# One tile for each score, more idle transposes at the start, and a written order for the end of an attention and expert layer

## The chip, the cores and the metric

The kernel runs on one core of one Trainium2 chip. A core has five engines that run at the same time and wait for one another through semaphores: TensorE (PE in the profile, with PEld for its weight loads), VectorE (DVE), ScalarE (ACT), GpSimd (POOL) and SyncE (SP), which here only issues transfers. The metric is device microseconds of one execution. Before the change the median of three runs is 1106.41 us (1105.07 to 1107.13).

## The reference

One sequence of S = 1024 rows of H = 512 numbers, all in 32-bit floats, goes through an attention layer and a feed-forward layer, each between two layer norms:

```
x = x + norm(attention(norm(x)))
x = x + norm(ffn(norm(x)))

attention: 32 query heads, 8 key/value heads of 128 numbers, causal;
           scores = q k^T / sqrt(128); softmax over the keys; times v; times w_o
ffn:       base = x base_W^T + base_b
           p    = softmax(x router_W^T + router_b)      (15 routes, the best 8 kept)
           w[e] = sum of the kept p whose route maps to expert e
           out  = base + 2 * sum over e of ((x A_e^T) * w[e]) B_e
```

A norm takes the mean and the variance of a row of 512 numbers.

## The kernel before, in words

The rows are cut into 8 row tiles t of 128, and the heads into 8 groups g (one key/value head and its four query heads). A block is one (g, t). There are 64 blocks: groups 0 to 5 one after the other, and then groups 6 and 7 in turn, with the row tiles in the order 0 1, 6 7, 4 5, 2 3. The main loop (lines 798 to 829) goes over the blocks. In block i it makes the four scores tiles (i, j), j = 0 to 3; each holds 32 query rows of all four heads (128 partitions) against the n = 128 t + 32 (j + 1) keys that causality leaves. Between the four, PE is given a quarter each of other work: projections for later blocks, the weighted values of block i - 2, the output projection of earlier ones, and pieces of the feed-forward layer of row tiles that are complete.

One score goes like this (scores, line 404). PE multiplies into a PSUM tile s. DVE adds the causal mask to the last 32 columns (L426) and takes the maximum (L428), ACT takes the exponential with its sum (L433). When the next score has been multiplied, DVE takes the reciprocal of the sum (L439), ACT scales (L440), and DVE transposes blocks of 32 x 32 (L446) into a tile T. After the fourth score, 16 transfers bring T into the key-major tile K (L106, to_keys), and two blocks later PE multiplies K with the values (po).

[...] The pool ps_s has two tiles s of 1024 columns, two banks each; ps_m has three banks under the tag pm, for every product and transpose but po, which has one bank of its own. A row tile with t below 4 needs at most 512 columns. There the kernel puts two scores into one tile:

```
if t < TPB and j % 2:
    s = score_tile.pop(0)[:, QB:]
else:
    s = ps_s.tile([P, S], F32, tag="s", name=f"s_{name}")
    score_tile[0] = s
```

The order on an engine is either written or planned. PE's instructions, the loads and those of DVE and ACT in the score chain are pinned to program order (keep). The other instructions are placed by the framework's planner. Function order (line 95) pins an instruction as long as the main loop runs (score_tile is then not empty) and leaves it to the planner afterwards. The vector work of a row tile (norms, routing) is cut into steps; in the main loop they are put into a list (defer) and worked off one or more per score (work_off). After the main loop defer carries each step out at once, so that its instructions follow directly in the program, and the planner orders them.

What is left behind the last scores (lines 832 to 848) is: the weighted values and output projections of the last two blocks, and the feed-forward layer of the row tiles c = 4, d = 5, e = 2 and f = 3. For each row tile it runs project_o (sum pO onto acc, L489), ffn_norms (statistics, norm, add of x, statistics, norm to h), ffn_router (transpose of h to hT, product pl with router and A, softmax over 15 routes, and the step route, which picks the best 8 and scales, L614 to L631), ffn_out (four products of hT with base_W into pf, transpose of the scaled hw, product with B, the sum y with the bias, L659, its norm, and the add to acc, L665), and the store. The reciprocal root of every norm is a power on POOL (L228) between two steps of DVE. In this part pl, and pf of e and f, lie in halves of the tiles s (bank_ffn); the other products take pm banks.

At the start x is loaded, normed row tile by row tile on DVE, transposed by PE (input_turn) and copied to xnT by ACT (L264); 20 transposes of the identity matrix (idle, line 771), whose result nobody reads, run on PE before x is there.

Of the kernel before, what the change touches and what calls it, by code (L numbers as in the profile page):

```python
# [22 lines left out]
def kernel(  # L23
# [68 lines left out]
    def keep(ins):  # L92
        return tc.keep_in_program_order(ins)

    def order(ins):

        return keep(ins) if score_tile else ins

    def matmul(*args, **kw):
        keep(nc.tensor.matmul(*args, **kw))  # L100
# [115 lines left out]
    def layernorm(dst, src, name, by=nc.vector):  # L216

        got = []

        def statistics():  # L220
            stats = small.tile([P, 6], F32, tag="stats", name=f"stats_{name}")
            order(nc.vector.bn_stats(stats, src))
            mv = small.tile([P, 2], F32, tag="mv", name=f"mv_{name}")
            order(nc.vector.bn_aggr(mv, stats))
            ve = small.tile([P, 1], F32, tag="ve", name=f"ve_{name}")
            order(nc.vector.tensor_scalar(ve, mv[:, 1:2], EPS, None, ALU.add))
            rstd = small.tile([P, 1], F32, tag="rstd", name=f"rstd_{name}")
            order(nc.gpsimd.tensor_tensor(rstd, ve, neg_half, ALU.pow))  # L228
            got.extend((mv, rstd))

        def norm():
            mv, rstd = got
            if by is nc.vector:
                order(by.tensor_scalar(dst, src, mv[:, 0:1], rstd, ALU.subtract, ALU.mult))
                return
            shift = small.tile([P, 1], F32, tag="shift", name=f"shift_{name}")
            order(nc.vector.tensor_scalar(shift, mv[:, 0:1], rstd, -1.0, ALU.mult, ALU.mult))
            nc.scalar.activation(dst, src, AF.Identity, bias=shift, scale=rstd)

        return statistics, norm  # L240

    def bank(name):
        return ps_m.tile([P, 512], F32, tag="pm", name=name)

    spare = []

    def bank_ffn(name):

        if not score_tile:
            if not spare:  # L250
                both = ps_s.tile([P, S], F32, tag="s", name=f"s_{name}")
                spare.extend((both[:, :512], both[:, 512:]))
            return spare.pop(0)
        return bank(name)

    def bank_pv(name):
        return ps_m.tile([P, 512], F32, tag="po", name=name, bufs=1)
# [1 line left out]
    def transposed(dst, src, name):  # L259

        pt = bank(f"ptx_{name}")
        for c in range(KC):
            transpose(pt[:, ts(c, P)], src[:, ts(c, P)], ident)
        nc.scalar.copy(dst, pt.rearrange("p (c q) -> p c q", q=P))  # L264

    def input_norms(rows):

# [110 lines left out]
    score_tile = {}  # L378
    deferred = []

    def defer(*steps, first=False):

        if score_tile:
            deferred[:0] = steps if first else ()
            deferred.extend(() if first else steps)
        else:
            for step in steps:
                step()

    def work_off(most=1):  # L390
        for _ in range(min(most, len(deferred))):
# [12 lines left out]
    def scores(g, t, j):  # L404

        n = t * P + (j + 1) * SQ
        full = (t + 1) * P
        name = f"{g}_{t}_{j}"

        if t < TPB and j % 2:  # L410
            s = score_tile.pop(0)[:, QB:]
        else:
            s = ps_s.tile([P, S], F32, tag="s", name=f"s_{name}")
            score_tile[0] = s
        for c0 in range(0, n, QB):
            w = min(QB, n - c0)
            matmul(
                s[:, c0 : c0 + w],
                qTs[g, t // 2][:, (t % 2) * NSUB + j, :, :].rearrange("p h q -> p (h q)"),
                kTs[g, c0 // QB][:, :w],  # L420
                start=True,
                stop=True,
            )
        pin = keep if blocks.index((g, t)) >= N2 + 2 else lambda ins: ins
        rescale_scores()
        keep(nc.vector.tensor_tensor(s[:, n - SQ : n], s[:, n - SQ : n], smask, ALU.add))  # L426
        nmax = small.tile([P, 1], F32, tag="nmax", name=f"nmax_{name}")
        keep(nc.vector.tensor_reduce(nmax, s[:, :n], AX.X, ALU.max, negate=True))  # L428
        p = act.tile([P, S], F32, tag="p", name=f"p_{name}", bufs=3)
        if n < full:  # L430
            nc.gpsimd.memset(p[:, n:full], 0.0)  # L431
        total = small.tile([P, 1], F32, tag="total", name=f"total_{name}")
        keep(nc.scalar.activation(p[:, :n], s[:, :n], AF.Exp, bias=nmax, accum_out=total))  # L433
        finish_scores()
        work_off(1 + len(deferred) // 5)

        def rescale():
            rec = small.tile([P, 1], F32, tag="rec", name=f"rec_{name}")
            keep(nc.vector.reciprocal(rec, total))  # L439
            keep(nc.scalar.mul(p[:, :n], p[:, :n], rec))  # L440

        def finish():
            if j == 0:
                turned[g, t] = turn_view(turn_tile("T", g, t), t)
            pin(
                nc.vector.transpose(  # L446
                    turned[g, t][:, :, j, :, :].rearrange("p b k q -> p k b q"),
                    p[:, :full].rearrange("p (k b q) -> p k b q", b=R, q=SQ),
                )
            )  # L450
# [17 lines left out]
    def weighted_values(g, t):  # L468


        def finish(po):
            o = act.tile([P, R * P], F32, tag="attnT", name=f"attnT_{g}_{t}", bufs=3)
            attnT[g, t] = o
            nc.scalar.copy(o, po)  # L474
            keyed.pop((g, t))

        def term(k):
            p = keyed[g, t][:, :, :, k, :].rearrange("p h s q -> p (h s) q")
            return vs[g // GV, k][:, ts(g % GV, D)], p

        return chained(
            lambda: bank_pv(f"po_{g}_{t}"), [lambda k=k: term(k) for k in range(t + 1)], finish
        )
# [88 lines left out]

    def ffn_norms(t):

        by = nc.gpsimd if score_tile else nc.vector
        statistics, norm = layernorm(acc[t], acc[t], f"a{t}")

        def add_x():
# [7 lines left out]
            norm_h()  # L586
            state["h", t] = h

        defer(statistics, add_x, statistics_h, last)

    def ffn_router(t):

# [4 lines left out]

        def products():
            hT = state["hT", t]
            pl = bank_ffn(f"pl_{t}")[:, : NR + ER]  # L600
            for c in range(KC):
                matmul(pl, hT[:, c, :], ra_sb[:, c, :], start=(c == 0), stop=(c == KC - 1))
            lg = small.tile([P, NR], F32, tag="lg", name=f"lg_{t}")
# [2 lines left out]
            order(nc.vector.tensor_reduce(nmax, lg, AX.X, ALU.max, negate=True))  # L606
            ex = small.tile([P, NR], F32, tag="ex", name=f"ex_{t}")
            total = small.tile([P, 1], F32, tag="total", name=f"totalr_{t}")
            nc.scalar.activation(ex, lg, AF.Exp, bias=nmax, accum_out=total)
            defer(lambda: route(pl, ex, total), first=True)  # L610

        def route(pl, ex, total):
            rec = small.tile([P, 1], F32, tag="rec", name=f"recr_{t}")
# [27 lines left out]
    def ffn_out(t):  # L641
# [2 lines left out]

        def base(c):
            if c == 0:
                pf.append(bank_ffn(f"pf_{t}") if t in (e, f) else bank(f"pf_{t}"))
            matmul(pf[0], state["hT", t][:, c, :], weights["base", c], start=(c == 0), stop=False)

        def turn_hw():  # L650
            pt = bank(f"ptw_{t}")
            transpose(pt[:, :ER], state.pop(("hw", t)).rearrange("p e r -> p (e r)"), ident)
            hwT = state["hwT", t] = ffn.tile([ER, P], F32, tag="hwT", name=f"hwT_{t}")
            nc.scalar.copy(hwT, pt[:, :P])

        def finish():
            matmul(pf[0], state.pop(("hwT", t)), bt_sb, start=False, stop=True)
            y = ffn.tile([P, H], F32, tag="hy", name=f"y_{t}", bufs=3)
            order(nc.vector.tensor_tensor(y, pf[0], bias_bc, ALU.add))  # L659
            by = nc.vector if t in (e, f) else nc.gpsimd  # L660
            statistics, norm = layernorm(y, y, f"y{t}", nc.vector if t in (e, f) else nc.scalar)

            def add_y():
                norm()
                order(by.tensor_tensor(acc[t], y, acc[t], ALU.add))  # L665
                state["done", t] = True

            defer(statistics, add_y)

        w = [(512, lambda c=c: base(c)) for c in range(KC)]  # L670
        return w[:2], [(P, turn_hw)], w[2:], [(512, finish)]
# [68 lines left out]
    def run(pieces):  # L740
        for _, f in pieces:
            f()
# [25 lines left out]
    input_norms(range(TPB, NT))  # L768

    idle = bank("idle")  # L770
    for n in range(20):
        transpose(idle[:, ts(n % KC, P)], ident, ident)
    input_turn(0)
    run(project_v(0, 0))
    for t in range(1, 3):
        input_turn(t)
# [54 lines left out]

    rescale_scores()
    finish_scores()
    score_tile.clear()
    work_off(len(deferred))
    for t in (e, f):
        reload_x(t)
    (turn_d, products_d), (turn_e, products_e), (turn_f, products_f) = map(ffn_router, (d, e, f))
    out_c, out_d, out_e, out_f = map(ffn_out, (c, d, e, f))
    o_pair = project_o_pair(*pairs[N // 2 - 2])  # L840
    run([turn_d] + weave(o_pair[:8], attend(N - 2)) + [products_d] + o_pair[8:])
    run(out_c[0] + out_c[1] + out_c[2] + attend(N - 1))
    run(project_o(*blocks[N - 2]) + out_c[3] + project_o(*blocks[N - 1]))
    run(out_d[0] + out_d[1] + out_d[2] + [turn_e] + out_d[3] + [products_e])
    run(out_e[0] + out_e[2][:1] + [turn_f] + out_e[2][1:] + [products_f])
    run(out_f[0] + out_e[1] + out_f[2][:1] + out_e[3] + out_f[2][1:] + out_f[1] + out_f[3])
    for t in (*ready, c, d, e, f):
        ffn_store(t)


# [39 lines left out]
```

## Time and profile before

| What | Before |
|---|---|
| median of three runs | 1106.41 us |
| profiled execution, its own time | 1105.28 us |
| span of the profile, first to last instruction | 1103.5 us |
| mean granted clock of TensorE | 0.994 |
| PE busy | 1074.5 us, 97% |
| DVE busy | 654.0 us, 59% |
| ACT busy | 491.2 us, 45% |
| POOL busy | 113.8 us, 10% |
| last DVE instruction ends | 1100.31 us |
| moved by DMA | 111.82 MB |

A row of a group or of the order in time names the source line, the engine, the operation and its tiles (written <- read), with the shape; [x <- y] says how long the engine stood idle before it and what ended that. Matmuls overlap, so their rows last longer than the distance from one start to the next, which is what counts for throughput: one 128x512 matmul row lasts 592 ns, and the next starts 429 ns after it. Each product of 32-bit numbers is two such rows. Helpers record under their own line: every product of PE is L100, every transpose L103, every transfer L106, so work is told apart by tile names.

### The profile page before, as it was taken

To read this page: it belongs to the slowest core of one execution; us is meant where nothing else is said; L and a number is where in the kernel's file an instruction comes from. 1 tells how busy PE (TensorE), PEld (TensorE's weight loads), DVE (VectorE), ACT (ScalarE), POOL (GpSimd) and SP (SyncE) were. 2 spreads that over 40 slices of the span, in tenths; PEclk is the share of its full clock that TensorE was granted. 3 is DMA by queue.
4 is the path that set the end of the run, shared out by engine and by line. 5 is a ranking of instruction groups with operands and counts; after the bars stand their busy time and mean duration, and the time that the engine had idled before them with its cause. 6 is when DMAs were issued, how large, how long until landed. Compare 5 with 4: busy or idle time off the path is not lost.

```text
span 1103.5 us, 12827 instructions
## 1 busy us (share of the span) xinstructions
PE 1074.5 (97%) x3836; PEld 704.5 (64%) x3836; DVE 654.0 (59%) x1529; ACT 491.2 (45%) x991; POOL 113.8 (10%) x299
## 2 busy tenths in 40 slices
PE   8899999999999999999999999999999999999895
PEld 6676666666776666656676666666777556466452
DVE  4466555765465545766456654765446766566746
ACT  2554534554354434554354443555335554453501
POOL 2400012000020002000020000100020110111212
PEclk9999999999999999999999999999999999999998
DMA  5145342455125431454224441365333655444221
GB/s 181 40 107 141 67 115 58 125 144 115 24 68 155 107 82 45 113 144 105 52 60 125 121 104 37 93 176 123 86 102 100 166 144 116 127 107 104 68 67 38
DMA packets 79061, 111.82 MB, mean 101 GB/s; under 512 B 18176, under 2 KB 50560, under 8 KB 78992
## 3 DMA queue, kind: packets, MB, share of 16 engines
q1 hardware_dynamic: 52976, 82.08, 31.5%
q10 hardware_dynamic: 25040, 27.27, 7.9%
q0 software_dynamic: 976, 1.65, 0.6%
q8 instruction: 31, 0.51, 0.2%
q14 instruction: 38, 0.31, 0.1%
HBM read 33.34 MB, written 2.10 MB: 32 GB/s over the span
## 4 chain that ended last, share of the span: by engine, by line
PE 82%; DVE 7%; ACT 5%; DMA 2%; issue 1%; SPq 1%; POOL 1%; ACTq 0%; POOLq 0%; DVEq 0%
PE po L100 20%; PE s L100 18%; PE pq L100 16%; PE pk L100 4%; PE pv L100 4%; PE pe L100 4%; PE pa L100 3%; ACT p L433 2%; PE pO L100 2%; PE pc L100 2%; PE pb L100 2%; PE pd L100 2%; DVE T L446 2%; PE pf L100 2%; DVE nmax L428 2%; ACT p L440 2%
## 5 line engine op out<-in xcount | busy, mean ns | idle before, releaser
L100 PE MATMUL s<-kT,qT 128*128 128x512 f32 (+15 forms) x768 | 273.8, 465 | 8.7 <-ACT p L433 8.6
L100 PE MATMUL po<-K,v 128*128 128x512 f32 x576 | 277.3, 596 | 4.3 <-DMA K<-T 2.6
L433 ACT ACTIVATE p<-s,nmax 128x32 f32<-128x32 f32 (+31 forms) x256 | 179.2, 700 | 203.1 <-DVE nmax L428 197.9
L440 ACT ACTIVATE p<-p,rec 128x32 f32<-128x32 f32 (+31 forms) x256 | 187.9, 734 | 179.3 <-DVE rec L439 121.0
L446 DVE STREAM_TRANSPOSE T<-p 128x128 f32<-128x128 f32 (+7 forms) x256 | 198.2, 775 | 100.4 <-ACT p L440 89.4
L100 PE MATMUL pq<-xnT,wq 128*128 128x256 f32 x1024 | 235.7, 379 | 0.0
L100 PEld LDWEIGHTS s<-kT,qT 128*128 128x128 f32 x768 | 144.0, 190 | 137.4 <-issue 105.5
L100 PEld LDWEIGHTS pq<-xnT,wq 128*128 128x128 f32 x1024 | 192.8, 190 | 38.5 <-issue 16.5
L428 DVE TENSOR_REDUCE nmax<-s 128x1 f32<-128x32 f32 (+31 forms) x256 | 180.6, 705 | 8.2
L100 PEld LDWEIGHTS po<-K,v 128*128 128x128 f32 x576 | 107.8, 191 | 78.0 <-issue 63.3
L426 DVE TENSOR_TENSOR s<-s,smask 128x32 f32<-128x32 f32 x256 | 47.8, 187 | 132.2 <-PE s L100 131.5
L431 POOL MEMSET p<- 128x96 f32 (+2 forms) x192 | 29.7, 155 | 848.4 <-DVE T L446 782.9
L439 DVE RECIPROCAL rec<-total 128x1 f32<-128x1 f32 x256 | 39.8, 155 | 55.1 <-ACT p L433 53.2
L100 PE MATMUL pv<-wv,xnT 128*128 128x256 f32 x256 | 69.1, 388 | 0.9 <-ACT xnT L264 0.9
L350 ACT ACTIVATE qT<-pq 128x512 f32<-128x512 f32 x64 | 38.1, 595 | 71.1 <-PE pq L100 71.1
L474 ACT COPY attnT<-po 128x512 f32<-128x512 f32 x64 | 37.4, 584 | 63.2 <-PE po L100 63.0
L100 PE MATMUL pk<-xnT,wk 128*128 128x512 f32 x128 | 64.5, 593 | 0.0
L100 PE MATMUL pa<-wo,attnT 128*128 128x256 f32 x224 | 62.7, 390 | 0.0
L100 PEld LDWEIGHTS pv<-wv,xnT 128*128 128x128 f32 x256 | 49.1, 194 | 11.0 <-issue 2.7
L100 PEld LDWEIGHTS pa<-wo,attnT 128*128 128x128 f32 x224 | 41.6, 192 | 19.4 <-issue 14.5
L433 ACT ACTIVATION_READ_ACCUMULATOR p<-s,nmax 128x1 f32 x256 | 49.5, 193 | 0.0
L523 DVE TENSOR_TENSOR sums<-attnT 128x256 f32<-128x256 f32 x28 | 11.9, 425 | 56.8 <-ACT attnT L474 56.7
(120 smaller groups left out, 776.6 us busy)
## 6 DMA issues: line engine op xcount, KB each, us to landing
K<-T SPq DMA_DIRECT2D x128, 128.0 KB, 2.4
K<-T SPq DMA_DIRECT2D x128, 112.0 KB, 2.2
wq<-in_w_q_dram ACTq DMA_DIRECT2D x27, 512.0 KB, 4.8
K<-T SPq DMA_DIRECT2D x128, 96.0 KB, 2.2
K<-T SPq DMA_DIRECT2D x128, 80.0 KB, 2.1
K<-T SPq DMA_DIRECT2D x123, 64.0 KB, 2.0
wo<-in_w_o_dram ACTq DMA_DIRECT2D x28, 256.0 KB, 3.8
K<-T SPq DMA_DIRECT2D x123, 48.0 KB, 1.9
```

The source lines that it names most:

```text
L100: keep(nc.tensor.matmul(*args, **kw))
L350: nc.scalar.mul(qTs[g, u][:, :, j - 1 : j + 1, :].rearrange("p s h q -> p h s q"), pm[0].rearrange("p (h s q) -> p h s q", h=2, q=SQ), scale,)
L426: keep(nc.vector.tensor_tensor(s[:, n - SQ : n], s[:, n - SQ : n], smask, ALU.add))
L428: keep(nc.vector.tensor_reduce(nmax, s[:, :n], AX.X, ALU.max, negate=True))
L431: nc.gpsimd.memset(p[:, n:full], 0.0)
L433: keep(nc.scalar.activation(p[:, :n], s[:, :n], AF.Exp, bias=nmax, accum_out=total))
L439: keep(nc.vector.reciprocal(rec, total))
L440: keep(nc.scalar.mul(p[:, :n], p[:, :n], rec))
L446: nc.vector.transpose(turned[g, t][:, :, j, :, :].rearrange("p b k q -> p k b q"), p[:, :full].rearrange("p (k b q) -> p k b q", b=R, q=SQ),)
L474: nc.scalar.copy(o, po)
L523: nc.vector.tensor_tensor(s1, a21, a22, ALU.add)
```

## The change

Three things change. First, every score has a tile s of its own, in all row tiles; the two-in-one branch goes, and with it the spare halves (bank_ffn): pl is now always a pm bank, and pf of e and f takes a whole tile s each. Second, there are 26 idle transposes before the first input_turn in place of 20, and 4 more right behind it, ahead of the first value projection. Third, the part behind the last scores gets a written order: order and several ACT instructions are now pinned there, steps are put into one list per row tile (held), and calls go(...) place each step at a chosen point between PE's pieces. With that, the norm of y for row tile e goes from DVE to ACT, and its add from DVE to POOL. The stores of the row tiles that are ready are issued ahead of this part, and not after it.

```diff
     def order(ins):
-        return keep(ins) if score_tile else ins
+        return keep(ins)
...
-            nc.scalar.activation(dst, src, AF.Identity, bias=shift, scale=rstd)
+            act_norm = nc.scalar.activation(dst, src, AF.Identity, bias=shift, scale=rstd)
+            if held:
+                keep(act_norm)
...
-    def bank_ffn(name):
-        if not score_tile:
-            if not spare:
-                both = ps_s.tile([P, S], F32, tag="s", name=f"s_{name}")
-                spare.extend((both[:, :512], both[:, 512:]))
-            return spare.pop(0)
-        return bank(name)
...
+    held = {}
+
+    def defer(t, *steps, first=False):
+
+        if held:
+            held[t].extend(steps)
+            return
+        deferred[:0] = steps if first else ()
+        deferred.extend(() if first else steps)
+
+    def go(*rows):
+
+        for t in rows:
+            held[t].pop(0)()
...
-        if t < TPB and j % 2:
-            s = score_tile.pop(0)[:, QB:]
-        else:
-            s = ps_s.tile([P, S], F32, tag="s", name=f"s_{name}")
-            score_tile[0] = s
+        s = ps_s.tile([P, S], F32, tag="s", name=f"s_{name}")
...
-        by = nc.gpsimd if score_tile else nc.vector
+        by = nc.vector if held else nc.gpsimd
...
-            pl = bank_ffn(f"pl_{t}")[:, : NR + ER]
+            pl = bank(f"pl_{t}")[:, : NR + ER]
...
-                pf.append(bank_ffn(f"pf_{t}") if t in (e, f) else bank(f"pf_{t}"))
+                if t in (e, f):
+                    pf.append(ps_s.tile([P, S], F32, tag="s", name=f"pf_{t}")[:, :512])
+                else:
+                    pf.append(bank(f"pf_{t}"))
...
-            by = nc.vector if t in (e, f) else nc.gpsimd
-            statistics, norm = layernorm(y, y, f"y{t}", nc.vector if t in (e, f) else nc.scalar)
+            by = nc.vector if t == f else nc.gpsimd
+            statistics, norm = layernorm(y, y, f"y{t}", nc.vector if t == f else nc.scalar)
...
-    for n in range(20):
+    for n in range(26):
         transpose(idle[:, ts(n % KC, P)], ident, ident)
     input_turn(0)
+    for n in range(4):
+        transpose(idle[:, ts(n, P)], ident, ident)
     run(project_v(0, 0))
...
-    score_tile.clear()
     work_off(len(deferred))
+    held.update({t: [] for t in (c, d, e, f)})
     for t in (e, f):
         reload_x(t)
+    for t in ready:
+        ffn_store(t)
...
     run([turn_d] + weave(o_pair[:8], attend(N - 2)) + [products_d] + o_pair[8:])
+    go(d)
     run(out_c[0] + out_c[1] + out_c[2] + attend(N - 1))
-    run(project_o(*blocks[N - 2]) + out_c[3] + project_o(*blocks[N - 1]))
-    run(out_d[0] + out_d[1] + out_d[2] + [turn_e] + out_d[3] + [products_e])
+    run(project_o(*blocks[N - 2]))
+    go(e)
+    run(out_c[3])
+    go(e, e)
+    run(project_o(*blocks[N - 1]))
+    go(e, f, c, f, f)
+    run(out_d[0] + out_d[1] + out_d[2] + [turn_e] + out_d[3])
+    go(f, c)
+    run([products_e])
+    go(d, e)
     run(out_e[0] + out_e[2][:1] + [turn_f] + out_e[2][1:] + [products_f])
-    run(out_f[0] + out_e[1] + out_f[2][:1] + out_e[3] + out_f[2][1:] + out_f[1] + out_f[3])
-    for t in (*ready, c, d, e, f):
+    go(d, f)
+    run(out_f[0] + out_e[1] + out_f[2][:1] + out_e[3])
+    go(e)
+    run(out_f[2][1:] + out_f[1])
+    go(e)
+    run(out_f[3])
+    go(f, f)
+    for t in (c, d, e, f):
         ffn_store(t)
```

The four remaining ACT copies of this part (hT, attnT, hwT and the exponential of the router) are pinned in the same way as act_norm.

More of the change, by code (lines that the diff above doesn't have):

```diff
@@ L243, in bank @@
         return ps_m.tile([P, 512], F32, tag="pm", name=name)
-    spare = []
-    def bank_ffn(name):
-        if not score_tile:
-            if not spare:
-                both = ps_s.tile([P, S], F32, tag="s", name=f"s_{name}")
-                spare.extend((both[:, :512], both[:, 512:]))
-            return spare.pop(0)
-        return bank(name)
     def bank_pv(name):
@@ L263, in transposed @@
             transpose(pt[:, ts(c, P)], src[:, ts(c, P)], ident)
-        nc.scalar.copy(dst, pt.rearrange("p (c q) -> p c q", q=P))
+        copy = nc.scalar.copy(dst, pt.rearrange("p (c q) -> p c q", q=P))
+        if held:
+            keep(copy)
     def input_norms(rows):
@@ L379 @@
     deferred = []
[L381 to L385, printed above, removed]
-        else:
-            for step in steps:
-                step()
+    held = {}
+    def defer(t, *steps, first=False):
+        if held:
+            held[t].extend(steps)
[5 more added lines that the diff above has]
+            held[t].pop(0)()
     def work_off(most=1):
@@ L408, in scores @@
         name = f"{g}_{t}_{j}"
-        if t < TPB and j % 2:
-            s = score_tile.pop(0)[:, QB:]
-        else:
-            s = ps_s.tile([P, S], F32, tag="s", name=f"s_{name}")
-            score_tile[0] = s
+        s = ps_s.tile([P, S], F32, tag="s", name=f"s_{name}")
         for c0 in range(0, n, QB):
@@ L473, in finish @@
             attnT[g, t] = o
-            nc.scalar.copy(o, po)
+            copy = nc.scalar.copy(o, po)
+            if held:
+                keep(copy)
             keyed.pop((g, t))
@@ L587, in last @@
             state["h", t] = h
-        defer(statistics, add_x, statistics_h, last)
+        defer(t, statistics, add_x, statistics_h, last)
     def ffn_router(t):
@@ L608, in products @@
             total = small.tile([P, 1], F32, tag="total", name=f"totalr_{t}")
-            nc.scalar.activation(ex, lg, AF.Exp, bias=nmax, accum_out=total)
-            defer(lambda: route(pl, ex, total), first=True)
+            act_exp = nc.scalar.activation(ex, lg, AF.Exp, bias=nmax, accum_out=total)
+            if held:
+                keep(act_exp)
+            defer(t, lambda: route(pl, ex, total), first=True)
         def route(pl, ex, total):
@@ L653, in turn_hw @@
             hwT = state["hwT", t] = ffn.tile([ER, P], F32, tag="hwT", name=f"hwT_{t}")
-            nc.scalar.copy(hwT, pt[:, :P])
+            copy = nc.scalar.copy(hwT, pt[:, :P])
+            if held:
+                keep(copy)
         def finish():
@@ L666, in add_y @@
                 state["done", t] = True
-            defer(statistics, add_y)
+            defer(t, statistics, add_y)
         w = [(512, lambda c=c: base(c)) for c in range(KC)]
```

## The prediction

> **What bounds the kernel now.** I read the page first. TensorE (PE) is busy 97% of the span, so the time is PE's work plus PE's idle moments, and a change that removes no PE work can only win idle moments.
>
> ```profile
> PE 1074.5 (97%) x3836; PEld 704.5 (64%) x3836; DVE 654.0 (59%) x1529; ACT 491.2 (45%) x991; POOL 113.8 (10%) x299
> PEclk9999999999999999999999999999999999999998
> ```
>
> Next the list of who waited for whom, for PE alone (total us, times, longest):
>
> ```profile
> PE s L100 <- ACT p L433: 8.6, 17, 1.2
> PE po L100 <- DMA K<-T: 2.6, 1, 2.6
> PE s_pf L100 <- ACT hT L264: 1.5, 1, 1.5
> PE ptx_x L103 <- DVE K_x L282: 1.3, 1, 1.3
> PE s_pl L100 <- ACT hT L264: 1.0, 1, 1.0
> PE ptw L103 <- DVE y L659: 0.9, 1, 0.9
> ```
>
> The largest is a score matmul waiting for an exponential. Asked by window, the same row says 3.2 us in 4 waits between 26 and 62 us (group 0), 4.7 in 12 from 62 to 1035, 0.7 in one after 1035. Which exponential? One wait in order of time (start, us):
>
> ```profile
> 153.29 1.03 PE L100 MATMUL pq<-xnT,wq 128*128 128x256 f32 x4
> 154.49 0.39 ACT L433 ACTIVATE p<-s,nmax 128x160 f32<-128x160 f32 x1
> 154.78 0.19 ACT L433 ACTIVATION_READ_ACCUMULATOR p<-s,nmax 128x1 f32 x1
> 155.03 0.59 PE L100 MATMUL s<-kT,qT 128*128 128x192 f32 x2 [0.71 <-ACT p L433]
> ```
>
> The score of 192 columns (t=1, j=1) starts 0.06 us after the exponential of 160 columns (t=1, j=0): the score just before it, which sits in the other bank of the same tile. I matched all 17 waits to their scores: every one is an odd j with t below 4, no other kind of score waits. So half a tile is given only when the other half's reader has ended.
>
> Then the start, by windows (us; stretch, PE busy with its count, PEld, DVE, ACT, POOL, granted clock, DMA share, GB/s):
>
> ```profile
> 5.40:6.70 1.30, 0.01 (x1) 0.00 (x0) 1.23 (x5) 0.57 (x1) 0.92 (x2) 1.00 1.03 363
> 6.70:8.00 1.30, 0.66 (x4) 0.42 (x4) 1.23 (x4) 1.29 (x2) 0.99 (x5) 1.00 1.08 316
> 8.70:11.30 2.60, 2.60 (x8) 2.06 (x7) 2.04 (x9) 0.00 (x0) 0.79 (x1) 0.50 1.08 369
> ```
>
> PE sits still for most of 5.4 to 8.06 and the clock then goes to 0.50 until 11.4. Last the end, DVE in order of time:
>
> ```profile
> 1075.19 0.55 DVE L234 TENSOR_SCALAR h<-acc,mv_h,rstd_h 128x512 f32<-128x512 f32 x1 [0.73 <-POOL rstd_h L228]
> 1075.65 0.68 DVE L659 TENSOR_TENSOR y<-pf,bias_bc 128x512 f32<-128x512 f32 x1
> 1076.26 0.68 DVE L489 TENSOR_TENSOR acc<-pO,acc 128x512 f32<-128x512 f32 x1
> 1082.78 0.55 DVE L234 TENSOR_SCALAR h<-acc,mv_h,rstd_h 128x512 f32<-128x512 f32 x1 [0.73 <-POOL rstd_h L228]
> 1087.06 1.27 DVE L626 TENSOR_TENSOR ws<-mexp,sel 128x120 f32<-128x120 f32 x1
> 1096.08 0.68 DVE L659 TENSOR_TENSOR y<-s_pf,bias_bc 128x512 f32<-128x512 f32 x1
> 1099.62 0.69 DVE L665 TENSOR_TENSOR acc<-y,acc 128x512 f32<-128x512 f32 x1
> ```
>
> After 1069 DVE, not PE, sets the pace: it stands idle 0.6 to 0.75 us before each norm (POOL's power is under way), though y of row tile c and the pO sum of f were ready at about 1070.4 and 1073.8 and ran only at 1075.65 and 1076.26.
>
> [...] 0.50 lasts about 3.4 us (8.0 to 11.4), again about 1049.2 to 1052.5 after 2.6 us of idle. [...] here the idle transposes alone took the clock up (213 ns apart until 4.5 us, 109 after), so the measurement decides: more of them can hold it. [...] ws took 1.27 us beside a POOL add, 0.28 without (1090.87).
>
> **The change part by part**, against the profiled execution (1105.28 us, span 1103.5; the median of the runs, 1106.41, is 1.1 above it).
>
> *Own tiles.* A wait costs more than its row shows: at 155.03 the four pq matmuls run 0.216 apart from 153.29, so PE could have issued at 154.15 and lost 0.88, where the row shows 0.71 (it counts from a modelled end); the second half of the score follows 0.10 late too. So 0.27 more each. From 62 to 1035: 4.7 + 12 x 0.27 = 7.9 us. Group 0: 3.2 + 4 x 0.27 = 4.3, plus two waits too short for the row, 0.5: 4.8. The one after 1035: 0.97, worth nothing, because PE then waits for the DMA of K at 1048.38, which follows from DVE's transpose of the block before and SP's 16 issues of 0.6 us, not from PE. What is late next: the score now waits for the exponential two scores back, in place of one (odd j) or three (even j). In groups 1 to 5 that ended over 2.9 us before every narrow score, so nothing comes back. In group 0 the smallest distance is 1.55 us (score at 46.09, exponential ended 44.53), and PE would run up to 4.8 us ahead of today while the chain exponential, reciprocal, mask, maximum, exponential can follow only so far: from 31.64 to 47.79 it made 7 steps of 2.3 us, and without waits needs about 1.9 (its instructions 1.4 to 1.7, plus ACT's copies of 0.6 in between) where PE wants 1.93. I take 4.0 (bounds 2 and 4.8). Other cover: K of block (1,2), which lands 1.1 us before PE asks, gets 0.6 less. Sum 11.9, bounds 7 and 12.7.
>
> *Idle transposes.* Six more at 0.109 fill 5.25 to 5.9, before x is ready at 6.68; four more at 0.109 lie inside the wait 7.4 to 8.06 for ACT's copy. At full clock both cost nothing; cold (0.213) the first would end at 7.05 and cost 0.4. What they may win: eight pv matmuls at 0.427 instead of 0.216 and a slow first one, 1.75 us. [...] 0 to 1.75; I take 1.7 on this execution. Behind it wq has landed by 12.4 and is wanted at 13.4, so it stays won.
>
> *The end in written order.* The PE order is untouched. With the rows' durations and 0.03 us between dependent steps (0.14 to POOL), DVE goes: sum of e, three statistics, to 1071.30; y of c under the power, to 1072.02; norm, add x, statistics, to 1074.43; sum of f under the power; h of e at 1075.73, as today, but y and the sum (1.2 us) are behind it. Then statistics of f and of y c (2.2), norm, add, statistics, y of d under the power, h of f at 1081.66 (today 1083.33). Shift c, router e, statistics of d, route of e (eight instructions, 1.84 plus gaps, and 0.4 behind POOL's add for c): 1085.9, today 1088.96. Route of f with ws held by the add for d (1.2): 1089.4, today 1091.79. y of e, statistics, power, shift, to 1092.2; y of f and its statistics, to 1094.0. POOL's add for e (after ACT's norm, 93.2 to 94.4) is now ahead of the last power, which costs 0.45. Power, norm, add: 1096.3, today 1100.31. Less 0.2 for locks: 3.8 (bounds -1 and 5). For e, norm and add (1.24) leave DVE for a shift of 0.21.
>
> pl now takes one of three pm banks and is held until the route's end, some 5 us; at each request I find another of the three already free (pf of c at 1058.88 can have pd's, free at 1058.1), so 0; if the bank handed over were pl's, 1.5 once. The early stores come behind the same reloads on SP as today: 0.
>
> Sum: 11.9 + 1.7 + 3.8 = 17.4; 1105.28 - 17.4 = 1087.9. The median of before lies 1.1 higher[...], so I say 1089.
>
> **Rivals.** *The score waits come back* at two back (17%): ACT, with its own copies between, becomes the bound of narrow blocks. For: group 0 is close. Against: distances of 2.9 and more elsewhere. Group 0 gives 0, the others half (4.0), plus 0.9 and 3.8: 8.7, 1097. *The written order hurts the end* (14%): DVE is in order, and the sum of f, waiting for pO, holds h of e; routes stand behind statistics. For: the add ahead of the last power. Against: each wait found under a power. Tail -1, body 11.9, start 0.9: 1094 to 1095. *The change doesn't do what it says* (5%): the wait belongs to something else of ACT's; then 0.9 + 3.8: 1101.7. *Slower* (5%): today an even score has three scores of distance, now two. There are 128 narrow scores; if every one then waited 0.16 us, 128 x 0.16 = 20 us would exceed all gains: 1109. It decides where the exponential comes 1.7 us later against PE than now at each narrow score (1.55 + 0.16); the distances of 2.9 speak against it.
>
> **How the numbers follow.** The forecast has 59%, own range 1084 (all upper bounds, 12.7 + 1.75 + 5 = 19.5, and a little) to 1092. The range takes in the first two rivals in most of their width: 1084 to 1096.5. About 2.2 us (0.2%) is what can be told from no change. All but the slower rival are faster by more, with 2% left for none: 0.93, 0.02, 0.05.
>
> **What would show it.** PE's row "s <- ACT p" falls from 8.6 to under 1; what is left is in group 0. The clock between 8.7 and 11.3 is 1.00. y of c and the sum of f run under a power; the last DVE add ends some 4 us sooner after the pO matmuls. The 2.6 us wait for K grows to about 3.5, and may cost or spare the half clock behind it, 1.7 us either way. The prediction is wrong if new waits for p, or for an ACT copy, stand in group 0, or if DVE's idle time at the end grows.

## The result, and the profile after

The changed kernel takes 1087.8 us, median of four runs (1086.82 to 1088.06), against 1105.74 (1104.09 to 1107.13) for the kernel before, measured beside it: a ratio of 0.9837, interval 0.982 to 0.9854. The forecast was 1089.0. The profiled execution took 1087.64 us with a span of 1085.9, which is 17.6 less than the 1103.5 before; the working had come to 17.4.

The page of the changed kernel, its lines of busy time and granted clock:

```profile
PE 1068.1 (98%) x3846; PEld 705.7 (65%) x3846; DVE 652.6 (60%) x1528; ACT 492.3 (45%) x992; POOL 115.0 (11%) x300
PEclk9999999999999999999999999999999999999998
```

PE's share rises by a point: PE does the same products and ten transposes more, and 17.6 us of other time are gone. Its waits, largest first (total us, times, longest):

```profile
PE po L100 <- DMA K<-T: 4.6, 1, 4.6
PE idle L103 <- POOL ident masks.py:199: 1.5, 1, 1.5
PE po L100 <- ACT attnT L468: 1.1, 3, 0.4
PE ptx_x L103 <- DVE K_x L275: 1.0, 2, 0.6
```

The row "s <- ACT p", 8.6 us before, is not there at all, in group 0 either. The waits for hT (1.5 and 1.0) and for y (0.9), all of the end, are gone too. The wait for K near the end has grown from 2.6 to 4.6, and is now the largest.

The start by windows (stretch, PE, PEld, DVE, ACT, POOL, granted clock, DMA share, GB/s):

```profile
5.40:6.70 1.30, 0.66 (x7) 0.43 (x5) 1.18 (x4) 0.40 (x1) 0.92 (x2) 1.00 1.00 365
6.70:8.00 1.30, 1.09 (x8) 0.86 (x8) 0.06 (x1) 1.29 (x2) 0.83 (x4) 1.00 1.05 314
8.70:11.30 2.60, 2.26 (x15) 1.79 (x14) 2.15 (x7) 0.96 (x2) 1.50 (x2) 1.00 1.07 373
```

PE works in the two stretches where it sat, and between 8.7 and 11.3 the clock is 1.00 where it was 0.50: the view counts 15 instructions of PE there in place of 8. The end, DVE in order of time:

```profile
1056.28 0.69 DVE L485 TENSOR_TENSOR acc<-pO,acc 128x512 f32<-128x512 f32 x1 [6.47 <-PE pO L100]
...
1058.02 0.68 DVE L663 TENSOR_TENSOR y<-pf,bias_bc 128x512 f32<-128x512 f32 x1
...
1061.17 0.68 DVE L485 TENSOR_TENSOR acc<-pO,acc 128x512 f32<-128x512 f32 x1
1061.98 0.55 DVE L234 TENSOR_SCALAR h<-acc,mv_h,rstd_h 128x512 f32<-128x512 f32 x1
...
1073.87 1.10 DVE L620 TENSOR_TENSOR sel<-pr,rest 128x15 f32<-128x15 f32 x1
...
1081.39 0.55 DVE L234 TENSOR_SCALAR y<-y,mv_y,rstd_y 128x512 f32<-128x512 f32 x1 [1.06 <-POOL rstd_y L228]
1081.97 0.69 DVE L669 TENSOR_TENSOR acc<-y,acc 128x512 f32<-128x512 f32 x1
```

y of c (1058.02) and the sum of f (1061.17) now run in the time of a power on POOL. Only 0.13 us stand idle before the norm to h (1061.98), where there was 0.73. From the sum of e (first line) to the end of the last add it is 26.38 us; the same stretch was 30.82 before (1069.49 to 1100.31).

The gain can be cut at marks that both traces have (us from the start of the span; group and row tile in brackets):

| Mark | Before | After | Gained in the stretch up to here |
|---|---|---|---|
| first score starts | 26.31 | 24.88 | 1.43 |
| first score of (0, 4) starts, end of the narrow blocks of group 0 | 63.09 | 56.79 | 4.87 |
| first score of (7, 2) starts | 1021.89 | 1008.37 | 7.22 |
| po of (7, 2) starts, behind the wait for K | 1048.38 | 1035.16 | -0.30 |
| DVE's sum of e starts | 1069.49 | 1056.28 | -0.01 |
| last DVE instruction ends | 1100.31 | 1082.66 | 4.44 |

### The profile page after: what moved, and what is told of

Read it like the earlier page. It is cut to its first block, busy times and chain, and to the rows that moved or that the text cites. A ratio compares the mean times of both kernels' runs of the same rounds, so it can differ in the third digit from the quotient of the medians.

```text
span 1085.9 us, 12864 instructions
## 1 busy us (share of the span) xinstructions
PE 1068.1 (98%) x3846; PEld 705.7 (65%) x3846; DVE 652.6 (60%) x1528; ACT 492.3 (45%) x992; POOL 115.0 (11%) x300
## 3 DMA queue, kind: packets, MB, share of 16 engines
q10 hardware_dynamic: 25040, 27.27, 7.9%
## 4 chain that ended last, share of the span: by engine, by line
PE 87%; DVE 5%; ACT 2%; DMA 2%; SPq 1%; POOL 1%; issue 1%; POOLq 0%; ACTq 0%; DVEq 0%
PE po L100 21%; PE s L100 19%; PE pq L100 18%; PE pk L100 5%; PE pv L100 4%; PE pe L100 4%; PE pa L100 4%; PE pO L100 2%; PE pc L100 2%; PE pb L100 2%; PE pd L100 2%; PE pf L100 2%; DVE T L440 1%; SPq L106 1%; DVE nmax L422 1%; ACT p L427 1%
## 5 line engine op out<-in xcount | busy, mean ns | idle before, releaser
L519 DVE TENSOR_TENSOR sums<-attnT 128x256 f32<-128x256 f32 x28 | 11.9, 424 | 56.5 <-ACT attnT L468 56.4
```

Source lines behind the costliest of these rows:

```text
L519: nc.vector.tensor_tensor(s1, a21, a22, ALU.add)
```

## The experiments

Times are medians of four executions, unless the text says that there was one. Differences of about 1 us between two kernels are at the edge of what the medians can tell, so where one is in dispute the stretch between two marks of the trace decides.

### The score tiles: own_only, pair_back, cross

own_only is the kernel before with one edit: own tiles, but the old start and the old end.

```diff
-        if t < TPB and j % 2:
-            s = score_tile.pop(0)[:, QB:]
-        else:
-            s = ps_s.tile([P, S], F32, tag="s", name=f"s_{name}")
-            score_tile[0] = s
+        s = ps_s.tile([P, S], F32, tag="s", name=f"s_{name}")
+        score_tile[0] = s
```

> The kernel before with one edit: a tile of its own for every score; start and end as before. My theory: the waits of odd narrow scores for the exponential just before them are the whole of the body's gain, and they need neither the start nor the end of the change. In the two traces the first 64 us won 6.3 us of which 1.4 lie ahead of the first score, so group 0 gave 4.9; groups 1 to 5 gave 7.2; 0.3 was lost at the K wait behind the last scores. Expected 1105.7 - 11.8 = 1093.9 us, and no wait of s for p in the list of waits. Rival: part of that gain came with the pinned order at the end (the planner places the vector work of the whole program anew): then 1096 us or more.

It took 1093.35 us (1091.82 to 1094.36), ratio 0.9886 (0.9871 to 0.99). The kernel before, measured beside it, took 1105.61: 12.3 us from this edit alone. Its first wait of PE:

```profile
PE po L100 <- DMA K<-T: 4.6, 1, 4.6
```

The row of the exponential is gone, and the wait for K is at 4.6 already: the longer wait comes from the tiles, not from the written end.

pair_back is the opposite: the changed kernel with the old branch for pairs put back.

```diff
-        s = ps_s.tile([P, S], F32, tag="s", name=f"s_{name}")
+        if t < TPB and j % 2:
+            s = score_tile.pop(0)[:, QB:]
+        else:
+            s = ps_s.tile([P, S], F32, tag="s", name=f"s_{name}")
+            score_tile[0] = s
```

> The full change with one part undone: two narrow scores share a tile again, as before. Theory: 1087.8 + 11.8 = 1099.6 us, with some 8 us of waits of s for p, all at odd j of narrow row tiles. Rival (the parts are not additive: once the start is faster the waits in group 0 change): more than 2 us off that.

1099.72 us (1098.69 to 1100.9), ratio 0.9945 (0.993 to 0.996). The waits come back, in the same number as in the kernel before. Most of what their sum has more (9.8 against 8.6) is a single wait of 1.8 that was 0.7 there:

```profile
PE s L100 <- ACT p L431: 9.8, 17, 1.8
PE po L100 <- DMA K<-T: 3.1, 1, 3.1
```

cross tells what it is about the pair that costs. Two scores share a tile again, but j with j + 2, not with j + 1. A second half then waits for the reader of the score two back, just as far as with own tiles.

```diff
-        s = ps_s.tile([P, S], F32, tag="s", name=f"s_{name}")
+        if t < TPB and j >= 2:
+            s = score_tile.pop(j - 2)[:, QB:]
+        else:
+            s = ps_s.tile([P, S], F32, tag="s", name=f"s_{name}")
+            score_tile[j] = s
```

> The full change, but narrow scores share tiles in another way: j = 0 and 1 take a tile each, j = 2 and 3 the second halves of these. Theory: what counts is how far back the wait reaches. A half is given when the reader of the other half has ended, here the exponential two scores back, the same as with tiles of their own: 1087.8 us within 1. Rival: sharing a tile costs in itself (two engines in neighbouring banks of one tile, or the tile's release): then near pair_back, 1099.6.

1088.01 us (1086.53 to 1088.48), ratio 0.984 (0.9824 to 0.9856), and no wait of a score: the same as the change. So sharing a tile as such costs nothing that these times can show; a wait that reaches only one score back is what cost 12 us. The three kernels were measured together: from pair_back to cross 11.7 us, from the kernel before to pair_back 5.9 for start and end, together 17.6.

### The start: own_start, idle20_0, idle4

own_start is own_only with 26 and 4 idle transposes.

```diff
-    for n in range(20):
+    for n in range(26):
         transpose(idle[:, ts(n % KC, P)], ident, ident)
     input_turn(0)
+    for n in range(4):
+        transpose(idle[:, ts(n, P)], ident, ident)
```

> The kernel before with own tiles and the new idle transposes, its end as before. Theory: the start wins what the clock lost, 1.4 us in the two traces [...], so 1092.5 us against own_only's 1093.9; what is left to the full change, 4.4 us, is the written order of the end. Rival: the gain ahead of the first score is taken back in group 0, where the softmax chain could be the bound: then the same time as own_only.

1093.22 us (1092.96 to 1093.58), ratio 0.9886 (0.9871 to 0.9901): no different from own_only, where 1.4 was expected. The traces, of one execution each, show two reasons. In own_only's profiled execution the 20 old transposes were enough: its first score starts at 24.55, not at 26.31. And own_start's profile lost at the other end, which still has the old order. The window of own_start where it happens (columns as above), and then one row of products in its order of time:

```profile
1076.00:1080.00 4.00, 4.00 (x8) 1.58 (x7) 1.73 (x9) 0.27 (x1) 0.00 (x0) 0.68 0.01 3
```

```profile
1075.29 3.59 PE L100 MATMUL s_pf<-wbase,hT 128*128 128x512 f32 x4 [0.50 <-DVE lg L601]
```

The same row in the kernel before:

```profile
1089.11 1.95 PE L100 MATMUL s_pf<-wbase,hT 128*128 128x512 f32 x4 [0.50 <-DVE lg L604]
```

Behind the same two gaps of PE (about 1.5 and 0.5 us) the clock fell once and held once. own_start's stretch from the sum of e to the last DVE instruction is 32.31 us; in own_only and before it is 30.82.

idle20_0 is the change with the old start (20 transposes, none behind the first input_turn); idle4 is the same edit with range(4).

```diff
-    for n in range(26):
+    for n in range(20):
         transpose(idle[:, ts(n % KC, P)], ident, ident)
     input_turn(0)
-    for n in range(4):
-        transpose(idle[:, ts(n, P)], ident, ident)
```

> The full change with 20 idle transposes and none behind the first input_turn, as before. The pair own_only and own_start showed no difference in time (1093.35 and 1093.22 us), and the profile of own_only kept the full clock at the start with 20. New theory: the idle transposes are worth something [...] so on the median 0 to 1.75 us: 1087.8 to 1089.6. Old theory (my prediction): always worth 1.4 to 1.7, so 1089.2 to 1089.5 and a clock of 0.50 between 8.7 and 11.3 us in the profile. A rival: they cost a little where the clock holds anyway, then 1087.5.

> The full change with 4 idle transposes ahead of the first input_turn and none behind it. To be read in the profile: the distance of the first pv matmuls and the start of the first score, 24.6 to 25.0 us in all profiles so far with 26 and 4, and 24.6, 26.3 and 27.3 in three with 20. Theory: [...] pv at 427 ns, first score at 27 us or later, so the idle transposes as such are worth some 2.5 us and 20 of them sometimes fall short. Rival: the start is bound by x and DVE: first score at 25 us.

idle20_0: 1088.99 us (1087.98 to 1089.52), ratio 0.9847 (0.983 to 0.9864), which the medians can't tell from the change. Its profiled execution starts the first score at 27.27, 2.4 later than the change. idle4, one execution, took 1089.64, and starts it at 27.32. The order of time of idle4 shows why:

```profile
8.52 3.78 PE L100 MATMUL pv<-wv,xnT 128*128 128x256 f32 x8 [0.68 <-ACT xnT L255]
```

The same row of the changed kernel:

```profile
8.23 1.99 PE L100 MATMUL pv<-wv,xnT 128*128 128x256 f32 x8 [0.44 <-ACT xnT L255]
```

Eight products take 3.78 us against 1.99: half rate. So the start depends on the execution. With 20 transposes the first score came at 24.55, 26.31 and 27.27 in three profiles; with 26 and 4 it came between 24.64 and 25.00 in all ten profiles that have them. All ten had the good case, so the edit is worth between about nothing and 2.5 us in one execution; by medians it showed 0.1 and 1.2, neither of them clear of the spread.

The entries of the clock in the traces show where 20 fall short, though not why. Before the first entry PE runs at half rate: the idle transposes start 0.213 us apart (0.109 behind it, in the kernel before), so that at this rate 20 of them are over at 6.0 us and 26 at 7.3. Full clock comes at 4.63 us in the kernel before and at 5.29 in own_only, but at 13.80 in idle20_0. In the ten with 26 and 4 it comes between 4.31 and 6.80. How much work it takes to bring the full clock was not shown.

### The end: ye_dve, pow_first

ye_dve gives the norm of y of e and its add back to DVE.

```diff
-            by = nc.vector if t == f else nc.gpsimd
-            statistics, norm = layernorm(y, y, f"y{t}", nc.vector if t == f else nc.scalar)
+            by = nc.vector if t in (e, f) else nc.gpsimd
+            statistics, norm = layernorm(y, y, f"y{t}", nc.vector if t in (e, f) else nc.scalar)
```

> The full change, with the norm and the add of y for row tile e on DVE as before (in the written order). To be read in the profile, from the start of the pO sum of e on DVE to the end of the last DVE instruction: 26.4 us in the full change. Theory: DVE gets 0.55 + 0.69 in place of a shift of 0.21 ahead of y of f, 1.03 us later; the last power no longer stands behind POOL's add, 0.35 us sooner: 27.0. Rival: POOL's add is the real bound at the end; then 26.1.

One execution, 1088.01 us. The stretch from the sum of e to the last DVE instruction is 27.11 us, against 26.38: moving e off DVE is worth 0.7. (In the nine profiles that have the new end unchanged the stretch is 26.37 to 26.40.) No run takes the rest of the new end apart, so that its order, and not the earlier stores or the banks of pl and pf, wins the other 3.7 is read from the step times further down.

pow_first puts the last power ahead of POOL's add for e.

```diff
-    go(e)
     run(out_f[3])
-    go(f, f)
+    go(f)
+    go(e)
+    go(f)
```

> The full change, but the norm and add of y for e are placed behind the statistics of y for f, so that POOL takes the last power ahead of its add. The same stretch in the profile: theory 26.4 - 0.35 - 0.13 (the shift no longer stands ahead of y of f) = 25.9 us, if the last norm and add on DVE then don't collide with POOL's add. Rival: they collide, DVE's two-input add waits for POOL's: 26.4 or more.

One execution, 1087.49 us; the stretch is 26.37, where 25.9 was expected. The order of time of DVE and of POOL:

```profile
1080.73 1.63 DVE L669 TENSOR_TENSOR acc<-y,acc 128x512 f32<-128x512 f32 x1
```

```profile
1080.53 1.28 POOL L669 TENSOR_TENSOR acc<-y,acc 128x512 f32<-128x512 f32 x1 [0.42 <-ACT y L238]
```

The power comes sooner, but now the two adds run beside each other, and DVE's takes 1.63 us in place of 0.69: what the earlier power won, this delay took.

### The wait for K: k_last and what followed

The largest wait left is for the K of block (7, 2), which SP brings with 16 transfers. k_last gives every third of them to POOL's queue, as the last block has it already.

```diff
-                alone = 3 <= blocks.index((g, t)) < N - 1
+                alone = 3 <= blocks.index((g, t)) < N - 2
                 to_keys(g, t, by=three[:1] if alone else three)
```

> The full change, with the 16 transfers of K for the last block but one, (7, 2), shared between SP and POOL (11 and 5) as for the last block; before they are all on SP. PE now waits 4.8 us for that K. Theory: SP's 16 issues of 0.6 us are what it waits for; five fewer land K 3.1 us sooner, the wait falls to about 1.7, and the half clock behind it (1.9 us lost on the next matmuls) may go too: 1087.8 - 3.1 to - 5.0 = 1083 to 1084.7. Rivals: POOL's five issues, 0.5 us each, hold up the powers of row tile d, and T of the last block comes later: nothing won or lost; or K of (7, 3) gates instead (it has 5.1 us in hand, which are used up): 1085.

1084.43 us (1084.23 to 1084.83), ratio 0.9808 (0.9789 to 0.9827): the best run of the change is 2 us above the worst of this. Its waits of PE, and a window behind the one for K:

```profile
PE po L100 <- ACT attnT L468: 2.8, 4, 1.7
...
PE pl L100 <- ACT hT L255: 1.4, 1, 1.4
```

```profile
1033.00:1037.00 4.00, 3.90 (x14) 2.37 (x13) 3.29 (x12) 0.72 (x1) 0.00 (x0) 1.00 0.00 0
```

What is left ahead of po is 1.7 us (the row names attnT; in k_late the same wait of 1.7 is put down to the transfers of K), and the clock behind it is 1.00; in the changed kernel the window from 1034 to 1038 has 0.68. From the first score of (7, 2) to its po it is 23.9 us now, against 26.8: 2.9 won. Nothing more is won behind po, where it takes 21.4 us to the sum of e, against 21.1: a new wait stands there at 1038.78, pl for hT, 1.4, and takes what the full clock gave. I thought that POOL's five transfers hold up the power of that row tile. k_late puts them behind it:

```diff
         work_off(1 + len(deferred) // 5)
+        while late:
+            late.pop(0)()
...
-                load(dst[ts(b, SQ), h], src[ts(h, SQ), b], by[(h * NSUB + b) % len(by)])
+                one = lambda h=h, b=b: load(
+                    dst[ts(b, SQ), h], src[ts(h, SQ), b], by[(h * NSUB + b) % len(by)]
+                )
+                if (g, t) == blocks[N - 2] and by[(h * NSUB + b) % len(by)] is nc.gpsimd:
+                    late.append(one)
+                else:
+                    one()
```

k_late_rec is k_late without the deferred vector steps behind the last score:

```diff
-        work_off(1 + len(deferred) // 5)
+        if (g, t, j) != (*blocks[-1], NSUB - 1):
+            work_off(1 + len(deferred) // 5)
```

k_seven is k_late_rec with seven of the sixteen transfers on POOL:

```diff
+                if (g, t) == blocks[N - 2]:
+                    three = (nc.sync, nc.gpsimd) * 7 + (nc.sync,) * 2
```

> As k_last, but the five POOL transfers of K(7, 2) are issued behind the vector steps of the same score, so behind the power of the norm to h of row tile d. In k_last POOL issued them from 1023.5 to 1026.0 us, that power came at 1026.0 where its input had been ready since about 1024.1, and PE later waited 1.4 us for hT of d. Theory: that wait goes, and K still lands with SP's eleven: 1084.4 - 1.4 = 1083.0. Rival: POOL's transfers land later than SP's now, or the wait for hT is set by ACT's copy: 1084.4 or more.

> k_late, and no deferred vector steps behind the last score, so that its reciprocal, scaling and transpose stand ahead of the routing of row tile c on DVE. In k_last these come at 1034.9, some 3 us after the sum is ready, and K of (7, 3) lands only 0.3 us before PE takes it. Theory: K of (7, 3) would gate PE next once other waits go; T comes 3 us sooner and the time is k_late's or up to 1 us less: 1082 to 1083. Rival: the routing of c, which moves 1 us later, holds PE in its place: slower than k_late.

> k_late_rec with seven of the 16 transfers of K(7, 2) on POOL in place of five. In k_last PE still lost 1.8 us before po of (7, 2). Theory: two SP issues of 0.6 us fewer, 1.2 us sooner, if POOL's seven (0.5 each from about 1024.8) land by 1030.5: 1.2 us less than k_late_rec. Rival: POOL becomes the later queue: no gain.

| Kernel | Median (runs) | Ratio to before (interval) |
|---|---|---|
| k_late | 1083.88 (1083.79 to 1084.56) | 0.981 (0.9791 to 0.9828) |
| k_late_rec | 1084.49 (1083.79 to 1085.25) | 0.9816 (0.9794 to 0.9838) |
| k_seven | 1083.57 (1082.89 to 1084.09) | 0.9805 (0.9787 to 0.9824) |

By these times none of the three can be told from k_last. In k_late the power starts earlier and pl still waits 1.4, so POOL's queue was not the cause. In k_late_rec that wait is gone, and another of nearly its size has come:

```profile
PE pc L100 <- DVE acc L553: 1.2, 1, 1.2
```

So the vector steps that were moved away were wanted just as soon at their new place. In k_seven the wait ahead of po falls to 0.8, and the stretch from the first score of (7, 2) to its po is 0.9 shorter than in k_late_rec, where 1.2 was expected; the medians differ by as much, but within their spread.

What holds hT up can be read from ACT in the trace of k_last:

```profile
1037.44 0.81 ACT L238 ACTIVATE y<-y,shift_y,rstd_y 128x512 f32<-128x512 f32 x1 [1.59 <-DVE shift_y L237]
1038.16 0.56 ACT L255 COPY hT<-ptx_h 128x512 f32<-128x512 f32 x1
```

PE has transposed h by 1029.1. ACT, idle for 1.59 us, copies it only behind the norm of y of row tile c, and that waits for a shift which DVE reaches at 1037.23, behind the other vector steps of c. In k_late ACT has the same order (1037.73 and 1038.45). No run turns it around, so this cause is read, not tested.

All four versions beat both kernels, by 21 to 22 us against the kernel before and by 3.3 to 4.2 against the change.

## Why the prediction was right, point by point

**Own tiles, 11.9 foretold.** own_only measured 12.3, and pair_back to cross 11.7. The reading of the waits held: the reader was that of the neighbour in the tile, and a wait did cost more than its row (0.27 more was forecast; the twelve waits from 62 to 1035, 4.7 us by their rows, gave back 7.7 in the mean of twelve profiles, which is 0.25 more each). The parts:

- Group 0: 4.87, just above the upper bound of 4.8, where I took 4.0. No wait of a score is left there, so the chain of DVE and ACT followed all the way and the margin that I kept back for it was not needed.
- From there to 1021: 7.2 in this profile, where I said 7.9. Over the twelve profiles that have no such wait (own_only, own_start, cross, the change, and the eight made from it that keep its tiles) the same stretch is 7.2 to 8.3 us shorter than in the profile of before, 7.7 in the mean. A part of the spread is the cover I named: K of block (1, 2). In own_only its po starts 1.38 us after the products of pa ahead of it (183.71 and 185.09), with nothing waited for, and the last transfer of K has landed at 184.59, 0.5 before: of the slack of 1.1 I had foreseen a loss of 0.6. In the changed kernel the two are 1.96 apart (184.44 and 186.40). PE has the same lead there; but one of SP's issues took 1.39 us in place of 0.59, and the last transfer landed at 186.12. Why that issue was slow is not shown.
- After 1021: nothing, as foretold. The wait for K swallowed what was gained before it. It grew to 4.6, where I had said 3.5. The waits of PE between 1021 and 1049 in the kernel before:

```profile
PE po L100 <- DMA K<-T: 2.6, 1, 2.6
PE s L100 <- ACT p L433: 0.7, 1, 0.7
PE po L100 <- ACT p L440: 0.5, 1, 0.5
```

  I counted the second row and missed the third: po of block (6, 3) waited, for the last transfer of its own K by the time of landing (1036.20, po at 1036.40; the row names a scaled p), and in the changed kernel it no longer does. Both come back in the wait for K. It made no difference to the time, since from the first score of (7, 2) to its po it is 26.5 us before and 26.8 after: the transfers set it.

**Idle transposes, 1.7 foretold on this execution.** The trace gives 1.43 up to the first score, with the clock at 1.00 as told. In the medians it doesn't show clearly (0.1 and 1.2), since the old start was not always slow. "0 to 1.75" was too narrow at the top: idle20_0 and idle4 start the first score 2.4 later than the change. There the clock was not lost at 8 us, it had never come up (the first entry in idle20_0 comes at 13.80), and that case I had not looked for. The range was my estimate. What the runs show of the idle transposes themselves: between 4 and 30 of them, with nothing else changed, the first eight products go from half to full rate, from 3.78 us in idle4 to 1.99.

**The written end, 3.8 foretold.** The stretch from the sum of e to the last add is 4.4 shorter. The list of times that I had worked out can be laid beside the trace (end of each step, us after the start of the sum of e; the 0.2 that I took off for locks, delays of DVE beside POOL's adds, is not in it):

| Step | Foretold | Measured |
|---|---|---|
| y of c | 2.53 | 2.42 |
| h of e | 6.24 | 6.25 |
| h of f | 12.17 | 11.85 |
| route of e | 16.41 | 15.89 |
| route of f | 19.91 | 19.64 |
| shift of e | 22.71 | 22.32 |
| statistics of y of f | 24.5 | 24.05 |
| last add | 26.8 | 26.38 |

The order of DVE is the forecast's, and most of the 0.4 comes at h of f and the route of e: two instructions that don't need each other start up to 0.12 us closer than the 0.03 of distance that I put between all. The delays of DVE beside POOL's adds were the right size (pr 0.85 in place of 0.23 and sel 1.10 in place of 0.17: 1.55 in all; I had 0.4 and 1.2), though they hit other instructions than the one I named. POOL's add ahead of the last power cost 0.33 (DVE idle 1.06 in place of 0.73; I said 0.45), and pow_first shows that it can't be had back by turning the two around. By times the end is worth more, 5.2 from own_start to cross: own_start's execution at half clock there, 1.5 us, is a part that I had not counted. With the written order only one gap of 0.4 is left in PE's last products, and the clock stayed at 1.00 up to 1078. Whether this half clock is also why own_only's median lies 1.5 above its profiled run is not shown: the mean granted clock of its four executions (0.994 or 0.995) doesn't tell them apart.

**The rivals.** Waits at two back didn't come in any of the kernels with own tiles, nor in cross; so the rival that ended slower, which needed them at the narrow scores, had nothing to stand on. The written order helped. The change did what it says. The errors that were left partly cancel: start -0.3, group 0 +0.9, the body -0.7, the end with its lead-in +0.3. By medians more cancels: the start gave 0.1 or 1.2 where I took 1.7, the end 5.2 where I took 3.8. That the sum, 17.9, is so near the 17.4 of the working is in part luck.

## What to carry to other kernels

In these kernels a tile of two banks is handed over as a whole: when half of it is given to a second user, that user waits for the reader of the first half, and a row of short waits (0.2 to 1.2 us in the kernel before) on a busy engine adds up. Pair users that are far apart in time, or give each its own tile; both were worth the same.

What an engine gains ahead of a transfer is only kept if the transfer's issue moves up with it, so look at each DMA's slack before adding gains up. Once the busiest engine runs freely, the late transfer is the next thing to mend: splitting one block's transfers over two queues gave 3.4 us by medians, of which 2.9 show at the wait itself, for one character.

Behind the last large product, where the vector engine sets the pace, a list of its instructions with their rows' durations foretold each step to about half a microsecond. The idle time under another engine's short step is what a written order can fill.

## What the runs showed of the hardware

- A granted clock of 1.00 in a view is not always a measured one: the views print 1.00 where the trace has no entry of the clock yet. In idle20_0 the first entry comes at 13.80 us. Up to there PE runs at half rate (eight products in 3.78 us, as in idle4), though the window from 8.7 to 11.3 says 1.00; the kernel before, whose first entry comes at 4.63, has 0.50 at the same place with the same products. A rate is better read from the distance of equal matmuls. The window of idle20_0:

```profile
8.70:11.30 2.60, 2.60 (x7) 2.07 (x8) 2.06 (x8) 0.00 (x0) 0.95 (x2) 1.00 1.08 370
```

- In the kernel before the clock was at half from 8.05 to 11.46 us and from 1049.11 to 1052.53, in the changed one from 1035.45 to 1038.86: 3.41 us each time, and full again behind it. Ahead of the first of these, PE was busy for 1.43 us of the stretch from 4.63 to 8.05; in the changed kernel, where the clock stayed at 1.00, for 2.53. The other two came behind the waits of 2.6 and 4.6 us for K; behind the wait of 1.7 in k_last it was 1.00 (1033 to 1037). No run was made to test how much work keeps the clock or brings it back.
- The same gaps in PE's work kept the clock in one execution and lost it in another. At the old end, behind the two gaps of 1.5 and 0.5 us, the same four rows of products took 3.59 us in own_start and 1.95 in the kernel before. What decided it was not shown.
- On DVE even an instruction of 15 columns is held up by an add on POOL: in the changed kernel sel took 1.10 us beside one (1073.87), and 0.17 without (1071.05).
